# Layer 0, first phase: transposes and g's matmuls on two PSUM banks in turn instead of one

## The chip, the cores and the metric

The program runs on one core of a Trainium2 chip. The metric is the device time of one execution in microseconds (us); the profile of one execution spans 3190.1 us. The engines are named as the profile names them: PE (TensorE, with PEld for its weight loads), DVE (VectorE), ACT (ScalarE), POOL (GpSimd) and SP (SyncE, which here only issues transfers). PSUM is the memory that PE's results land in. The kernel uses eight banks of it, each a piece of 128 partitions by 512 float32 values.

## The reference

The input is 1024 images of 16 x 16 pixels with 16 channels, all in float32. Four layers follow one another, and each has the form x = x + f(groupnorm(x)), with eight groups of two channels.

```python
x = x + _L0_conv_ref(_gn(x), core0, core1, core2)   # a 4096 x 4096 matrix as a train of three cores
x = x + _L1_conv_ref(_gn(x), ...)                    # depthwise taps, dense 48 -> 128 -> 16, masks
x = x + _L2_conv_ref(_gn(x), ...)                    # 3 x 3 convolution, 16 -> 16
x = x + _L3_conv_ref(_gn(x), ...)                    # as layer 1, with other weights
```

Only layer 0 is touched by the change. Its matrix is given by three cores of ranks 1, 16, 16, 1: with `r` and `q` the inner ranks, each entry is a sum over r and q of core0[o0,i0,r] * core1[r,o1,i1,q] * core2[q,o2,i2]. The kernel forms the product of core1 and core2 once, calls it g, and then multiplies g with combinations of core0 to get the blocks of the matrix.

## The kernel before, in words

**Batches.** The 1024 images are worked in two halves of 512, n = 0 and n = 1. A tile "line" is 128 partitions (places and channels of an image) by 512 images, so it fills one bank as a matmul's result.

**Layer 0's main work.** `layer_train` computes the matrix product as a block product with seven products in place of eight (`PRODUCTS`, with sums and differences of blocks on both sides). It goes through five phases of 16 units each. A unit is one group of 128 output rows; it has some of the seven products, and each product is four matmuls of 128 x 128 by 128 x 512 that add up in one bank `po` (line 1078). Phase 0 has only two products for each unit, since only the half n = 0 is loaded and normalized when it begins; phase 1 has the five others, and the remaining phases have seven. Each product is cut in two steps, `go(0)` and `go(2)`, so phase 0 has 16 x 2 x 2 = 64 steps. Around its matmuls a step also calls work on the next units:

- `build(u + 1)` in the first step of unit u: eight matmuls from `gq` (a piece of g, from DRAM) and `R` (core0's combinations) into four banks `pw`, which ACT copies into the weights `w` (lines 1001 and 1006). DVE then forms a mixed block (line 1019).
- `store(u - 1)` and `gload(u + 2)`: transfers on SP's queue, the second brings a piece of g.
- `gather`: in phase 0 an ACT copy of `po` into `r` (line 1103).

**What is done beside phase 0.** The other half of the input must be turned: `turn` (line 821) makes four transposes of 128 x 128 into one bank `ptin`, ACT copies the bank to SBUF (lines 824 and 832), and POOL issues the transfer of the result to `xr` in DRAM. 18 such groups of the half n = 0 are left over at the start of phase 0, and 32 of n = 1 follow. Between them stand eight groups of `gs` (line 551): four matmuls into one bank `pg` that make a part of g, and an ACT copy (line 555). Two groups of `spread` (line 870, bank `ptmr`) bring the mean and the factor of the norm of n = 1 into place. POOL also issues the loads of the images of n = 1 into the slots that the turned pieces leave, in two lots of four transfers of 1 MB.

**Order.** [...] `run` emits the 64 steps of phase 0 and deals the work beside them between them by shares, so a group of transposes stands at a fixed place between two groups of matmuls on PE. ACT works in the same order of emission. [...]a group that writes into a bank waits until ACT's copy of what stood there before is done.

**Banks.** Until the end of layer 0 the eight banks are divided by tags: three for `po` (tag "o"), four for the builder (tag "w") and one shared bank (tag "m").

```python
stage(es, dict(gn, w=2, r=2, gq=2, R=1), dict(o=3, w=4, m=1))
```

The banks of a tag are given out in a ring: a new tile takes the one that was taken longest ago. The transposes and g's matmuls in phase 0 all take tag "m", so each group needs the bank of the group just before it. Before phase 0 begins (turning the first lines, g's first half) the same helpers use tag "w" alone. A build takes all four banks "w".

**Later.** Phases 1 to 4 follow, with the preparation of the weights of layers 1 and 3 (`nca_weights`, names `L_conv_...`) beside phase 1, and then layers 1 to 3. The change reaches none of their code.

A remark on counts: a float32 matmul of the code appears as two records in the trace, a transpose as one. A step's two matmuls are "po x4" in the trace, a build's eight are "pw x16", a group of g's four "pg x8", and a group of transposes "ptin x4".

Of the kernel before, what the change touches and what calls it, by code (L numbers as in the profile page):

```python
# [103 lines left out]
def conv_preact_kernel(ctx: ExitStack, tc: tile.TileContext, a: dict, out: bass.AP):  # L104
# [22 lines left out]
    def stage(es, sb, ps):  # L127

        for key, sizes, kw in (("sb", sb, {}), ("ps", ps, {"space": PSUM})):
            p = es.enter_context(  # L130
                tc.tile_pool(name=f"{key}{len(pool)}", bufs=1, reuse_waits="tile", **kw)
            )
            pool[key] = p, sizes
        pool[len(pool)] = None

    def work(shape, tag, name, dt=F32):
        p, sizes = pool["sb"]
        return p.tile(shape, dt, tag=tag, name=name, bufs=sizes[tag])

    def bank(shape, tag, name):  # L140
        p, sizes = pool["ps"]
        return p.tile(shape, F32, tag=tag, name=name, bufs=sizes[tag])

    def psum(shape, name):
# [342 lines left out]
    def train_setup(room):  # L487

        c1t = room[0:16, 0:4096].rearrange("p (h i w a k) -> p h i w a k", h=2, i=S, w=4, a=2)
        ra = [room[0:16, 4096 + 512 * a2 : 4608 + 512 * a2].rearrange("p (s m b f) -> p s m b f", s=2, m=2, b=2) for a2 in range(2)]  # L490
        c0 = room[0:16, 5888:6144].rearrange("p (i o) -> p i o", o=S)
        c1n = work([P, 2, NB], "t4", "core1")[:, 0].rearrange("p (t f) -> p t f", t=2)
        r = work([P, NB], "n", "cores")
        c2 = r[0:16, 0:256]
        c0n = r[:, 256:288].rearrange("p (t k) -> p t k", t=2)

        core1 = a["L0_conv_core1"].rearrange("k o i q -> o k (i q)")
        for h in range(2):
            for wv in range(4):
                for a2 in range(2):  # L500
                    A.dma_start(c1n[32 * wv + 16 * a2 : 32 * wv + 16 * a2 + 16, h], core1[8 * a2 + 4 * h + wv])
        A.dma_start(c2, a["L0_conv_core2"].rearrange("r o i k -> r (o i k)"))
        A.dma_start(
            c0n, a["L0_conv_core0"].rearrange("r o i k -> (r o i) k").rearrange("(t p) k -> p t k", p=P)
        )

        def cores():
            for h in range(2):
                for i2 in range(0, S, 4):
                    pt = bank([16, 4, P], "w", "pc1")  # L510
                    for j in range(4):
                        T.transpose(pt[:, j], c1n[:, h, 16 * (i2 + j) : 16 * (i2 + j) + 16], ident)
                    A.copy(c1t[:, h, i2 : i2 + 4].rearrange("p i w a k -> p i (w a k)"), pt)
            pt = bank([16, 2, P], "w", "pc0")
            for t in range(2):
                T.transpose(pt[:, t], c0n[:, t], ident)
            for t in range(2):
                A.copy(
                    c0[:, :, 8 * t : 8 * t + 8].rearrange("p i o -> p o i"),
                    pt[:, t].rearrange("p (o i) -> p o i", i=S),  # L520
                )

        def sums():
            c = c0.rearrange("p (b s t) o -> p s b (t o)", b=2, s=2)
            for a2 in range(2):
                G.memset(ra[a2], 0.0)
                G.tensor_copy(ra[a2][:, :, a2], c)
                G.dma_start(c_dram[a2], ra[a2].rearrange("p s m b f -> p (s m b f)"))

            st0["R"] = work([P, 2, 256], "R", "R")  # L530
            for g in range(4):
                G.dma_start(
                    st0["R"][32 * g : 32 * g + 32].rearrange("p s f -> p (s f)"),
                    c_dram.rearrange("a k f -> (a k) f"),
                )

        def gs(h, ih, o, ni, tag):


            if (h, ih, o) not in st0:  # L540
                if ih:
                    g = work([P, 2, NB], "t4", "g")
                else:
                    if o == 0:
                        st0["gw"] = work([P, 28, P], "w", "g")
                    g = st0["gw"][:, 8 * o : 8 * o + 8]
                st0[h, ih, o] = [g.rearrange("p m f -> p (m f)").rearrange("p (o f) -> p o f", o=8), 0]
            g, i2 = st0[h, ih, o]
            pg = bank([P, ni, 8, S], tag, "pg")
            for j in range(ni):  # L550
                T.matmul(
                    pg[:, j], c1t[:, h, 8 * ih + i2 + j].rearrange("p w a k -> p (w a k)"),
                    c2[:, P * o : P * o + P], start=True, stop=True,
                )
            A.copy(
                g[:, :, 16 * i2 : 16 * (i2 + ni)].rearrange("p o (j i) -> p j o i", j=ni), pg
            )
            st0[h, ih, o][1] += ni
            if i2 + ni == 8:
                nc.sync.dma_start(  # L560
                    g_dram[ih, 2 * h : 2 * h + 2, :, :, 8 * o : 8 * o + 8].rearrange(
                        "w v k o f -> (w v k) o f"
                    ),
                    g,
                )

        def all_gs(ih, tag):
            return [
                (1, lambda h=h, o=o: gs(h, ih, o, 4, tag)) for h in range(2) for o in range(2) for _ in range(2)
            ]  # L570

        return [cores, sums] + all_gs(0, "w"), all_gs(1, "m")

# [308 lines left out]
    def normed(p, n, src=None):  # L884

        X, E = part_tile(p)

        def op(b, t, k):
            x = X[:, b, t : t + 2, n]
            y = x if k or src is None else X[:, b, t : t + 2, src]  # L890
            m = mr[:, k, n].unsqueeze(1).broadcast_to([P, 2, NB])
            V.tensor_tensor(x, y, m, ALU.mult if k else ALU.subtract)  # L892

        return [(1.2, lambda b=b, t=t, k=k: op(b, t, k)) for b in range(2) for t in (0, 2) for k in range(2)]
# [34 lines left out]
    def part_steps(p):  # L929
        steps = load_part(p) + [10] + normed(p, 0) + normed(p, 1)  # L930
        return steps + combined(p, True) + combined(p, False)
# [528 lines left out]
    def steps_of(*more):  # L1460
        return (lambda: None), [x for m in more for x in m]

    def now(steps):
        for step in steps:
            step = step[1] if isinstance(step, tuple) else step
            if callable(step):
                step()
# [8 lines left out]
    with ExitStack() as es:  # L1476
        stage(es, dict(gn, w=2, r=2, gq=2, R=1), dict(o=3, w=4, m=1))
        setup, later = train_setup(XN[0].rearrange("p n b -> p (n b)")[:, 8192:14336])
        tag = ["w"]
        loads, stat, lines, tail = input_steps(0, tag, 0, nc.sync)  # L1480
        now(loads)

        A.activation(work([P, NB], "n", "warm")[:, 0:1], ident[:, 0:1], AF.Sqrt)
        now(setup[:1])
        now(stat[0] + stat[1])
        now(setup[1:])
        now(lines[0][:4] + lines[1][:4] + tail[:3] + lines[0][4:10] + tail[3:])
        start, phases = layer_train()
        start()
        now(normed(0, 0, 1) + combined(0, True))  # L1490
        tag[0] = "m"
        late = lines[0][10:] + lines[1][4:]
        loads, stat, lines, tail = input_steps(1, tag, 2, G)
        woven_in = [x for j in range(2) for i in range(4) for x in stat[j][i : i + 1] + lines[j][4 * i : 4 * i + 4]]
        run(
            steps_of(phases[0]), 130, (),
            (late[:6] + loads[0:4] + late[6:] + loads[4:] + later + woven_in + tail + normed(0, 1) + combined(0, False), 0.0, 1.0),
        )
        run(
            steps_of(phases[1]), 350, (),  # L1500
            (beside(make1, make3), 0.0, 0.74), (part_steps(1), 0.75, 0.98),
        )
        for i in (2, 3):
            run(
                steps_of(phases[i]), 415, (), (part_steps(i), 0.05, 0.9),
                ([lambda: conv.update(s=conv_weights()), 60, lambda: conv["s"]()] if i == 2 else [0.0], 0.0, 0.5),
            )
        nst, N = parts_cw(X0, True)
        for q in range(4):
            bg = alone(N, q - 1) if q else [0.0]  # L1510
            if q == 3:
                bg = bg + rstd(nst, slice(0, 96)) + [3] + scaled(N, range(3))
            run(
                steps_of(phases[4][56 * q : 56 * q + 56]), 104, [put(L1)] if q == 3 else (),
                (bg, 0.08, 0.95),
            )
# [66 lines left out]
```

## Time and profile before

| | |
|---|---|
| time, median of 3 runs | 3199.57 us (3197.21 to 3203.37) |
| span of the profiled execution | 3190.1 us |
| PE busy | 3058.5 us (96%) |
| DVE busy | 1785.6 us (56%) |
| ACT busy | 1018.3 us (32%) |
| POOL busy | 670.6 us (21%) |
| mean granted clock of PE | 0.98 of full |
| first matmul `po` of phase 0 | starts at 46.67 us |
| last transpose `ptin` | starts at 200.8 us |
| first transposes for phase 1's norm, `ptmr` of n = 1 | 210.32 us |

PE is the engine to watch: a microsecond in which it stands idle counts, as long as nothing else would have stopped it later. PEclk in the profile is the clock that the chip granted to PE. "Idle before" in a view is the time in which an engine stood still ahead of an instruction, with the instruction on another engine that ended the wait.

### The profile page before, as it was taken

What the parts mean: (1) busy time and instruction counts of PE and PEld (TensorE: products, weight loads), DVE (VectorE), ACT (ScalarE), POOL (GpSimd) and SP (SyncE); (2) the same over time, 40 slices, a digit from 0 to 9 for tenths busy, and PEclk for the clock granted to TensorE, in tenths of its full rate; (3) what the DMA queues carried; (4) which work ended last, traced back from release to release, by engine and by line L of the source; (5) the groups of instructions that cost most, each with busy time, mean ns of one, the idle gap of its engine ahead of it and who ended that gap; (6) DMA issues with size and microseconds to landing.
All of it is one profiled execution on the core that took longest, in us unless ns stands there. A gap on an engine that the chain in (4) does not pass through costs nothing.

```text
span 3190.1 us, 37179 instructions
## 1 busy us (share of the span) xinstructions
PE 3058.5 (96%) x13874; PEld 1260.3 (40%) x13874; DVE 1785.6 (56%) x2378; ACT 1018.3 (32%) x1690; POOL 670.6 (21%) x706
## 2 busy tenths in 40 slices
PE   7899899999999999999999999999979899999996
PEld 5444333444444444444444433333323233333332
DVE  5255345755554555544556678558757647754222
ACT  4331221100001000000111166666624356655553
POOL 1116532200000000000000034435432124432221
PEclk8999999999999999999999999999989999999998
DMA  7535545443333433322222254454476765433445
GB/s 283 201 142 97 121 101 160 133 144 104 104 109 132 146 116 104 104 98 96 90 95 90 76 168 133 129 167 154 139 192 110 185 139 173 136 92 115 128 137 186
DMA packets 243299, 424.77 MB, mean 133 GB/s; under 512 B 37844, under 2 KB 91952, under 8 KB 239408
## 3 DMA queue, kind: packets, MB, share of 16 engines
q1 hardware_dynamic: 217824, 368.63, 35.5%
q0 software_dynamic: 24480, 53.48, 8.3%
q8 instruction: 110, 1.80, 0.2%
q14 instruction: 69, 0.57, 0.1%
q10 hardware_dynamic: 816, 0.30, 0.0%
HBM read 238.78 MB, written 165.60 MB: 127 GB/s over the span
## 4 chain that ended last, share of the span: by engine, by line
issue 46%; PE 31%; POOL 8%; DMA 4%; DVE 2%; SPq 1%; ACT 1%; POOLq 0%; DVEq 0%; ACTq 0%
PE ph L1410 11%; PE po L1078 10%; PE po L1263 4%; POOL res L1313 4%; POOL u L1312 4%; PE po L1160 2%; DMA xn<-xf 1%; PE L_conv_pe L382 1%; SPq L941 1%; DVE xn L621 1%; DMA hx<-xn 1%; PE pw L1001 1%; PE ptout L948 1%; DVE sq L592 1%; POOL L_conv_wy L394 0%
## 5 line engine op out<-in xcount | busy, mean ns | idle before, releaser
L1078 PE MATMUL po<-xn,w 128*128 128x512 f32 x3584 | 1584.3, 598 | 4.6 <-DVE xn L892 4.6
L1078 PEld LDWEIGHTS po<-xn,w 128*128 128x128 f32 x3584 | 669.9, 190 | 852.6 <-issue 833.7
L1413 ACT ACTIVATE hid<-ph,pack 128x512 f32<-128x512 f32 x1024 | 653.9, 686 | 429.2 <-PE ph L1410 308.4
L1114 DVE TENSOR_TENSOR r<-r,po 128x512 f32<-128x512 f32 x576 | 377.8, 683 | 499.0 <-PE po L1078 476.3
L1312 POOL TENSOR_TENSOR u<-u,mask 128x512 f32<-128x512 f32 x128 | 202.5, 1582 | 1858.9 <-DMA nx<-xn 1241.7
L1410 PE MATMUL ph<-xn,wq 32*128 32x512 f32 x3664 | 573.1, 613 | 1.5 <-DMA wq<-L_conv_wy 1.5
L1006 ACT COPY w<-pw 128x512 f32<-128x512 f32 (+1 forms) x320 | 150.6, 558 | 1194.0 <-issue 970.4
L1410 PEld LDWEIGHTS ph<-xn,wq 32*128 32x128 f32 x3664 | 228.6, 184 | 263.3 <-issue 231.4
L1410 PE MATMUL ph<-xn,pack 32*128 32x512 f32 x1288 | 302.2, 631 | 4.5 <-ACT hid L1413 3.2
L1263 PE MATMUL po<-hid,pack 128*32 128x512 f32 x2048 | 283.0, 609 | 1.2 <-DVE u L1275 0.9
L1019 DVE TENSOR_TENSOR w<-w 128x512 f32<-128x512 f32 x320 | 211.2, 684 | 115.2 <-ACT w L1006 114.7
L621 DVE TENSOR_TENSOR xn<-xn,m 128x1024 f32<-128x1024 f32 x160 | 225.9, 1461 | 47.1 <-ACT m L636 47.1
L1313 POOL TENSOR_TENSOR res<-res,u 128x512 f32<-128x512 f32 x128 | 215.2, 1681 | 17.0 <-PE po L1263 2.7
L1275 DVE SCALAR_TENSOR_TENSOR u<-po,pack,xn 128x512 f32<-128x512 f32 x128 | 95.9, 749 | 157.6 <-PE po L1263 150.9
L1160 PE MATMUL po<-xn,convw 128*128 128x512 f32 x368 | 168.5, 609 | 0.0
L1410 PEld LDWEIGHTS ph<-xn,pack 32*128 32x128 f32 x1288 | 114.5, 187 | 100.7 <-issue 61.7
L1114 DVE TENSOR_TENSOR xn<-xn,po 128x512 f32<-128x512 f32 x96 | 64.3, 684 | 125.9 <-PE po L1078 125.8
L592 DVE TENSOR_TENSOR sq<-sq 128x1024 f32<-128x1024 f32 x78 | 110.6, 1418 | 15.2 <-ACT sq L606 12.0
L1263 PEld LDWEIGHTS po<-hid,pack 128*32 128x32 f32 x2048 | 42.9, 108 | 189.7 <-issue 137.4
L394 POOL DMA_DIRECT2D L_conv_wy<-xn x160 | 89.0, 563 | 99.0 <-ACT xn L152 90.7
L1160 PEld LDWEIGHTS po<-xn,convw 128*128 128x128 f32 x368 | 69.3, 193 | 99.3 <-issue 96.7
L592 DVE TENSOR_TENSOR s<-s,xn 128x1024 f32<-128x1024 f32 x60 | 86.4, 1441 | 29.1 <-DMA xn<-xf 27.9
(163 smaller groups left out, 1776.9 us busy)
## 6 DMA issues: line engine op xcount, KB each, us to landing
xf<-r SPq DMA_DIRECT2D x112, 512.0 KB, 3.8
xn<-xf SPq DMA_DIRECT2D x96, 512.0 KB, 5.1
r<-xf SPq DMA_DIRECT2D x80, 512.0 KB, 4.5
wq<-L_conv_wy SPq DMA_DIRECT2D x192, 192.0 KB, 2.8
res<-xf SPq DMA_DIRECT2D x128, 256.0 KB, 3.0
xf<-res SPq DMA_DIRECT2D x96, 256.0 KB, 2.0
res<-xr SPq DMA_DIRECT2D x256, 64.0 KB, 2.8
xf<-conv POOLq DMA_DIRECT2D x64, 256.0 KB, 6.1
```

The lines of the kernel that those rows point to most:

```text
L592: return lambda: V.tensor_tensor(st["t"], st["t"], p(), ALU.add)
L621: V.tensor_tensor(part, part, m().unsqueeze(1).broadcast_to([P, 2, NB]), op)
L1006: A.copy(w[:, k0:4, :, 32 * r : 32 * r + 32].rearrange("p k t (v o) -> p v (k t) o", v=2), pw[r],)
L1019: V.tensor_tensor(w[:, k], w[:, x], w[:, y], ALU.add if sign > 0 else ALU.subtract)
L1078: T.matmul(po, st["w", u][:, matrix, t], x, start=t == 0, stop=t == 3)
L1114: V.tensor_tensor(r[at], r[at], po, ALU.add if sign > 0 else ALU.subtract)
L1160: T.matmul(st["po", h][wh], conv["fw"][:, y], X[:, 16 * wh + h + y - 1], start=y == max(0, 1 - h), stop=y == min(2, S - h),)
L1263: T.matmul(po[32 * j : 32 * j + 32], nca["w1"][:, v], hid[j], start=v == 0, stop=v == 1)
L1312: G.tensor_tensor(u, u, st["m"][:, w2], ALU.mult)
L1313: G.tensor_tensor(r, r, u, ALU.add)
L1410: T.matmul(ph, w, x, start=k == 0, stop=k == len(tiles) - 1)
L1413: A.activation(h, ph, AF.Relu, bias=nca["bt"][:, r : r + 1])
```

## The change

The helper `bank` gets a new tag "mw". A request for it flips a counter and takes, in turn, one of the builder's four banks (tag "w") and the shared bank (tag "m"); the first request gets "w". The groups of `turn`, `spread` and `gs` that run beside phase 0 ask for "mw" instead of "m". So two groups in a row no longer need the same bank, and the second can be written while ACT copies the first. No bank, instruction or transfer is added or taken away, and the order on each engine stays.

```diff
+    either = [0]
+
     def bank(shape, tag, name):
         p, sizes = pool["ps"]
+        if tag == "mw":
+            either[0] ^= 1
+            tag = "mw"[either[0]]
         return p.tile(shape, F32, tag=tag, name=name, bufs=sizes[tag])
@@
-        return [cores, sums] + all_gs(0, "w"), all_gs(1, "m")
+        return [cores, sums] + all_gs(0, "w"), all_gs(1, "mw")
@@
         now(normed(0, 0, 1) + combined(0, True))
-        tag[0] = "m"
+        tag[0] = "mw"
         late = lines[0][10:] + lines[1][4:]
```

The builder's groups still ask for "w", and the preparation of the later layers' weights (`psum`) still for "m".

## The prediction

> **What bounds the kernel now.** I read the page first, then PE's waits in the stretch of phase 0, then PE's and ACT's timelines side by side, and last the transfers and the chain of waits behind the stretch.
>
> ```profile
> PE 3058.5 (96%) x13874; PEld 1260.3 (40%) x13874; DVE 1785.6 (56%) x2378; ACT 1018.3 (32%) x1690; POOL 670.6 (21%) x706
> ```
>
> PE stands idle for only 131.6 us of 3190.1. What phase 0 has of that (46 to 225 us) the waits of PE name:
>
> ```profile
> PE ptin L821 <- ACT lines L832: 13.5, 17, 1.2
> PE po L1078 <- DVE xn L892: 4.6, 1, 4.6
> PE pg L551 <- ACT g L555: 2.9, 4, 0.7
> PE ptin L821 <- ACT xn L824: 2.6, 3, 1.2
> PE pw L1001 <- DMA gq<-g_dram: 0.9, 1, 0.9
> ```
>
> Columns: total us, times, longest. Three rows are waits for the copy out of the shared bank: 13.5 + 2.9 + 2.6 = 19.0 us in 24 waits, 0.6% of the time. PE's timeline shows the two kinds:
>
> ```profile
> 125.33 0.73 PE L1001 MATMUL pw<-R,gq 32*128 32x128 f32 x16
> 125.99 0.66 PE L821 MATMUL ptin<-ident,xn 128*128 128x128 f32 x4
> 127.82 0.66 PE L821 MATMUL ptin<-ident,xn 128*128 128x128 f32 x4 [1.18 <-ACT xn L824]
> 128.31 1.88 PE L1078 MATMUL po<-xn,w 128*128 128x512 f32 x4
> 130.03 0.60 PE L821 MATMUL ptin<-ident,xn 128*128 128x128 f32 x4
> 130.47 3.60 PE L1078 MATMUL po<-xn,w 128*128 128x512 f32 x8
> 133.90 0.60 PE L821 MATMUL ptin<-ident,xn 128*128 128x128 f32 x4
> 135.23 0.66 PE L821 MATMUL ptin<-ident,xn 128*128 128x128 f32 x4 [0.73 <-ACT lines L832]
> ```
>
> And ACT's in the same place:
>
> ```profile
> 126.07 1.20 ACT L1006 COPY w<-pw 128x256 f32<-128x256 f32 x4 [1.72 <-PE pw L1001]
> 127.13 0.63 ACT L824 COPY xn<-ptin 128x512 f32<-128x512 f32 x1
> 128.51 0.59 ACT L824 COPY xn<-ptin 128x512 f32<-128x512 f32 x1 [0.75 <-PE ptin L821]
> ```
>
> The reader is to see that the group at 127.82 starts 0.06 us after the copy of the bank's former content ends (127.13 + 0.63 = 127.76), that ACT was late there because the builder's four copies stood before it, and that ACT is idle most of the time. A group that stands alone between `po` matmuls (130.03) waits for nothing.
>
> [...] 0.7 us gaps at every second group that follows another, none elsewhere. [...] from 102 to 122 us the granted clock by stretches of 4 us is 0.78, 0.80, 0.63, 0.50, 0.59, and a `po` x4 there takes 2.85 us instead of 1.88. That is where `pg` groups stand close together.
>
> **The change, part by part.**
>
> *Removed: the waits.* The idle time understates a wait, since the next group also loses its overlap with the one before. I count start to start. Unhindered, a group takes 0.44 us to the next start (130.03 to 130.47).
> - Second group of a pair, nothing before it: 14 times, steps of 1.27 to 1.37 us (133.90 to 135.23), minus 0.44: 0.83 to 0.93 each, 12.3 us in all.
> - Second group right behind a build: steps of 1.88, 1.83, 1.83, 1.83 and 1.64 (125.99 to 127.82), minus 0.44: 6.8 us.
> - g's pairs: 1.87 (95.42 to 97.29) against 1.08 unhindered (97.29 to 98.37): 0.8 each, four times, 3.2 us.
> - One group at 81.85, whose predecessor's copy waited for a transfer: 0.5 us.
>
> Sum 22.8 us; and after a blocked group the next `po` starts 0.05 us later (0.49 against 0.44), some 20 times, 1 us more: 23.8 us.
>
> *Added: waits on the builder's bank.* Requests alternate and the first gets "w", so I number the 58 groups through the timeline: odd ones get "w". The ring of "w" gives a group right behind a build the bank `pw` just written first. That bank is free at 126.07 + 0.39 (one of the four copies, median 386 ns) + 0.05, so 1.2 us after the build's start, where the group could start at 0.66: 0.53 us of wait. It hits the groups that now start at 50.68, 107.04, 138.19, 149.01 and 194.69: 5 x 0.53 = 2.7 us. Where the pair's second group gets "w" (79.11, 127.82) it could start 0.66 + 0.44 = 1.10 us behind the build: 0.1 us each. Behind the waiting group on PE only the next group and `po` are queued, and those are counted.
>
> *Moved to the builder.* A build takes all four "w" banks. The youngest was written by a group with at least one `po` x4 (1.72 us) in between; its copy ends about 0.7 + 0.6 us after the group. I cost this at nothing, hidden by `po`.
>
> *ACT.* A unit's copies are 1.2 (weights) + 2 x 0.58 (`r`) + at most six of 0.59, under 6 us in a unit that takes about 10: not a bound. `po` has three banks, so a late `r` copy stops nobody.
>
> *What transfers take back.* From 66 to 82 us the transfer engines' share is 1.0 and about 400 GB/s: POOL has issued four 1 MB loads at 61.92, behind PE's groups. The pieces `gq` of the build at 75.45, issued at 63.16, take up to 12.3 us and hold PE by 0.88. Loads and `gq` are issued behind PE's progress, and before them only 1.44 + 0.88 + 0.88 - 0.53 = 2.7 us are won; the landing moves forward by that, PE would by 2.7 + 1.8. The difference, 1.8 us, is lost. The turned lines' store issued at 69.02 lands after 12.1 us and holds ACT's copy at 81.21, but the second bank lets PE go on past it: the next "w" is free, and the next "m" is copied within 0.2 us. In the later stretches `gq` takes 2 to 4 us and is issued more than 8 us ahead, except at 118.98 (4.1 us ahead, with 2.9 at most), so I take 0.2 us there.
>
> *Sum.* 23.8 - 2.7 - 0.2 - 1.8 - 0.4 = 18.7 us at the end of phase 0.
>
> *Does it reach the end?* From 205 to 320 us PE has no wait. Then comes one of about 10 us; the chain leads there from PE:
>
> ```profile
> 317.97 1.01 PE L_conv_pe L382 x4
> 318.98 0.02 issue
> 319.00 0.02 ACTq L152
> 319.02 0.32 issue
> 319.34 0.59 ACT xn L152
> ...
> 353.62 1.93 PE L_conv_pe L382 x4
> ```
>
> In between POOL and its transfers work, but they were started by PE's matmul at 317.97, and POOL's earlier work at 281.35 by a DVE step that PE paces. So the whole chain comes earlier by the same amount. DVE's norm of n = 1 starts behind `ptmr` (PE, 210.32), and its last combination is ready at 236.0 where phase 1's third product needs it at about 239: both hang on PE's order and shift alike. Later stages are bound by PE or started by it. I take the full 18.7 us off 3199.6: 3181 us.
>
> **The rivals.**
> 1. *The gain as summed:* 3181 us. For it: all 24 waits are seen at their instruction. Against it: the count of residuals leans on a numbering by hand.
> 2. *The clock comes back too.* 20 us at a mean clock of 0.66 lose 20 x 0.34 = 6.8 us. Without the gaps, `po` has 1.72 of 3.9 us in g's pairs instead of 1.72 of 4.7[...]. Against it: a build and a pair of g make 2.9 us with few rows at work in one piece. If all of it goes: 3174 us.
> 3. *It is absorbed.* Transfers hold back everything between 61 and 82 us (5.3 us instead of 1.8), half-clock windows fall worse[...], and the chain through POOL at 320 to 353 doesn't shift. For it: POOL and the transfer queues are dense there. 12 us left without the last, near 0 with it: 3188 to 3200, with 3195 its middle.
> 4. *Slower.* If the ring made every build wait for the last groups' copies (16 x 0.7 = 11 us) and every "w" group for the builder's (29 x 0.53 = 15 us), 26 us would stand against 23.8: with the transfers' 1.8, 3204 us. Against it: only five groups stand right behind a build with "w".
>
> **How the numbers follow.** Chances: first 0.64, second 0.14, third 0.14, fourth 0.08. Faster by over 0.2% means below 3193.2: the first two and a third of the third, 0.82; within 0.2% 0.10; slower 0.08. The range goes from 3170 (second rival, with 3 us as the spread of the time of before) to 3193.
>
> **What would show it.** In the profile after: waits of `ptin` and `pg` for their own copies gone from PE; five of about 0.5 us on `w<-pw` copies in their place; the wait for `gq` at about 72 us grown to 2.5; the last `ptin` near 182 us and `ptmr` near 192 instead of 210.32; from there PE's records as before, shifted by 18 to 19 us, the POOL chain too. If `ptmr` comes early and the end doesn't, the third rival holds; if `pw` waits for `lines` copies at each build, the fourth; if `po` x4 at about 95 to 110 us takes 1.88 throughout, the second.

## The result and the profile after

| | before | after |
|---|---|---|
| time, median | 3198.39 us (3197.07 to 3203.37, 4 runs) | 3175.27 us (3171.91 to 3180.46, 4 runs) |
| ratio, with its 95% interval | | 0.9926 [0.9908, 0.9945] |
| span of the profiled execution | 3190.1 us | 3175.4 us |

The change takes 23 us off. The two profiled executions differ by only 14.7: the one of the kernel before is among its faster ones (3191.8 us as a run), and the two lost unlike amounts to a lower clock, as shown below. In the changed kernel the lines of code behind line 140 have moved by five (821 is 826, 1001 is 1006, 1006 is 1011, 1078 is 1083).

PE's busy time on the page is the same to 0.7 us, and so is the number of its instructions. So it isn't work that went, but waiting:

```profile
PE 3057.8 (96%) x13874; PEld 1262.0 (40%) x13874; DVE 1784.3 (56%) x2378; ACT 1016.6 (32%) x1690; POOL 669.9 (21%) x706
```

PE's waits between 46 and 225 us, columns as before (total, times, longest):

```profile
PE po L1083 <- DVE xn L897: 4.6, 1, 4.6
PE pw L1006 <- DMA gq<-g_dram: 2.4, 2, 1.4
PE ptin L826 <- ACT w L1011: 1.8, 4, 0.5
PE pg L556 <- ACT w L1011: 0.4, 1, 0.4
```

The 24 waits for a copy of `ptin` or `pg`, 19.0 us, are all gone. Five short ones for the builder's copies have come in their place, and the wait for the transfer of `gq` has grown from 0.9 to 2.4. PE's timeline shows what became of the place that the prediction looked at:

```profile
119.34 0.73 PE L1006 MATMUL pw<-R,gq 32*128 32x128 f32 x16
120.00 1.17 PE L826 MATMUL ptin<-ident,xn 128*128 128x128 f32 x8
121.01 1.88 PE L1083 MATMUL po<-xn,w 128*128 128x512 f32 x4
122.72 0.60 PE L826 MATMUL ptin<-ident,xn 128*128 128x128 f32 x4
123.16 3.60 PE L1083 MATMUL po<-xn,w 128*128 128x512 f32 x8
126.60 1.04 PE L826 MATMUL ptin<-ident,xn 128*128 128x128 f32 x8
127.47 1.88 PE L1083 MATMUL po<-xn,w 128*128 128x512 f32 x4
129.28 0.73 PE L1006 MATMUL pw<-R,gq 32*128 32x128 f32 x16
130.45 1.09 PE L826 MATMUL ptin<-ident,xn 128*128 128x128 f32 x8 [0.44 <-ACT w L1011]
```

The pair behind a build (120.00) is now one piece of eight transposes, 1.0 us from its start to the next `po` instead of 2.3. The pair at 126.60 takes 0.9 instead of 1.8. At 130.45 a pair whose first group has the builder's bank waits for the first `pw` copy.

**Two clocks.** The trace also records the time in which PE had half its clock (0.50 granted). A `po` x4 that lies in it takes 3.50 us instead of 1.88 (at 78.75 us in the change). To compare like with like I take the stretch from the first `po` of phase 0 to the second group of `ptmr` of n = 1, and subtract half of the half-clock time in it ("at full speed"); the rest is from there to the end, treated alike. This is an estimate: it takes PE as working all through the half-clock time. Both kernels were profiled three times:

| profile | stretch | half clock in it | at full speed | rest at full speed |
|---|---|---|---|---|
| before | 166.6 | 16.6 | 158.3 | 2929.0 |
| before, second | 169.2 | 22.9 | 157.8 | 2929.2 |
| before, third | 169.5 | 23.1 | 157.9 | 2927.0 |
| change | 151.8 | 26.4 | 138.6 | 2930.0 |
| change, second | 151.8 | 26.4 | 138.6 | 2929.5 |
| change, third | 151.8 | 26.3 | 138.6 | 2929.7 |

At full speed the stretch is 19.4 us shorter (158.0 - 138.6), the same in every pairing to 0.5 us, and the rest is what it was. The time lost to half clock comes on top. For the two profiled executions as a whole, half-clock time is 129.9 us before and 137.5 after: at full speed they are 18.5 us apart, and 3.8 us of that went to half clock, which leaves the 14.7.

### The profile page after: what moved, and what is told of

The parts are those of the page before. It is cut to its first block, busy times and chain, and to the rows that moved or that the text cites. A ratio compares the mean times of both kernels' runs of the same rounds, so it can differ in the third digit from the quotient of the medians.

```text
span 3175.4 us, 37193 instructions
## 1 busy us (share of the span) xinstructions
PE 3057.8 (96%) x13874; PEld 1262.0 (40%) x13874; DVE 1784.3 (56%) x2378; ACT 1016.6 (32%) x1690; POOL 669.9 (21%) x706
## 4 chain that ended last, share of the span: by engine, by line
issue 46%; PE 37%; POOL 7%; DMA 4%; DVE 2%; SPq 2%; ACT 1%; POOLq 0%; DVEq 0%; ACTq 0%
PE ph L1415 12%; PE po L1083 11%; PE po L1268 4%; POOL u L1317 3%; POOL res L1318 3%; PE po L1165 3%; DMA xn<-xf 1%; PE L_conv_pe L387 1%; SPq L946 1%; PE pw L1006 1%; PE ptin L826 1%; PE po L1174 1%; PE ptout L953 1%; DVE sq L597 1%; DVE xn L626 1%
```

## The experiments

Ratios are to the kernel before, measured beside each. Only the edits against the changed kernel are shown; e7 and e10 start from the kernel before.

**e1: the change again.** No edit.

> The changed kernel once more. If the gain is the removed waits alone (18.7 us as summed), the ratio to before is about 0.994. If half-clock windows of PE come back as a rule, it stays at 0.992 to 0.993 and its profile shows fewer half-clock windows in phase 0 than the kernel before (16.6 us of them between the first po and the second ptmr of n = 1); if they only fall by chance, their number in phase 0 differs from the first profile of the change (26.6 us). From the first po to the second ptmr group of n = 1: 166.6 us in the kernel before, 151.8 in the first profile of the change; after taking off half of the half-clock time, both theories want 138 to 139.

3173.95 us, 0.9932 [0.9917, 0.9947]. The stretch at full speed is 138.6 us as expected, with 26.4 us of half clock at the same places. So the half-clock times in phase 0 belong to this kernel and aren't chance, but they are more than before, not fewer: the gain isn't made by them.

**b1, b2, a1: both kernels again.** No edit.

> The kernel before, profiled again. PE's waits between the first po and the last ptmr are the same to 0.2 us (13.5, 2.9, 2.6 and 0.9 us); half-clock time there is 13.7 us or more at g's pairs (95 to 122 us) if g's pairs with gaps are its cause, and near 0 there if it falls by chance.

> As b1: a third profile of the kernel before, for how often half-clock windows stand at g's pairs with their gaps, and at 76 us behind the wait of 0.9 us for gq (none in the first).

> A third profile of the change. If the wait of 2.4 us for gq causes it, a half-clock window of 3.4 to 6.8 us stands behind that wait again, and one of up to 10.2 us at g's third pair, behind the wait of 0.44 us for the builder's copies.

One run each: 3187.12 and 3196.65 us for the kernel before, 3177.36 for the change. The waits repeat to 0.2 us but for the main `ptin` row, which is 12.7 and 12.8 instead of 13.5. At g's pairs (92 to 122 us) the mean clock is 0.77, 0.80 and 0.80 in the kernel before and 0.83 in all three profiles of the change. Behind the wait for `gq` (70 to 86 us) it is 1.00, 0.89 and 0.89 before, and 0.79 in all three of the change. Around the first build of phase 0 half clock lasts 6.8 us in the three profiles of before (42.78 to 49.61 us in the first of them), and 10.2 in the three of the change (44.45 to 54.69 in the first), where a wait of 0.49 us for the builder's copies stands right behind that build. The change thus loses less clock at g's pairs and more at the two other places.

**e4 and e5: each part alone.**

e4 leaves g's matmuls on the shared bank:

```diff
-        return [cores, sums] + all_gs(0, "w"), all_gs(1, "mw")
+        return [cores, sums] + all_gs(0, "w"), all_gs(1, "m")
```

e5 leaves the transposes there:

```diff
-        tag[0] = "mw"
+        tag[0] = "m"
```

> Only the transposes take two banks in turn; g's matmuls stay on the shared bank. Sum of the waits: 22.8 - 3.2 = 19.6 us of start-to-start time removed, so the time is about 3 us above the change and 15.5 us below before (ratio 0.995). In the profile four waits of pg for ACT's copy of about 0.7 us are back. If the clock windows around g's pairs hang on those gaps, it is up to 5 us above the change.

> Only g's matmuls take two banks in turn; the transposes stay on the shared bank. 3.2 us of waits removed, less one wait of 0.5 us behind a build: ratio 0.999. The transposes' waits stay at 13.5 + 2.6 us as before. If the clock comes back when g's pairs close up, half-clock time at 95 to 120 us falls below 13.7 us and up to 6 us more is gained (ratio 0.997).

e4: 3181.10 us, 0.9949 [0.9931, 0.9966]; at full speed 141.1 us, 2.5 more than the change. e5: 3188.09 us, 0.9969 [0.9956, 0.9981]; at full speed 154.6, 3.4 less than before. The parts (16.9 and 3.4) add up to 20.3 against 19.4 for both together. e4 shows its four `pg` waits of 2.9 us as expected, e5 its transposes' waits. e5 gains more than its waits: its interval lies below the 0.999 that those alone would make. Its clock at 92 to 122 us is 1.00, where the three profiles of before and e4 have 0.77 to 0.80. The stretches there:

```profile
70.00:86.00 16.00, 12.36 (x63) 6.54 (x61) 0.69 (x1) 6.18 (x13) 2.19 (x3) 1.00 0.91 356
92.00:122.00 30.00, 27.12 (x106) 15.94 (x106) 6.63 (x18) 8.69 (x19) 1.34 (x3) 0.77 0.67 253
```

(before), and of e5:

```profile
70.00:86.00 16.00, 13.03 (x58) 7.43 (x59) 0.69 (x1) 5.41 (x13) 2.20 (x3) 0.89 1.00 398
92.00:122.00 30.00, 28.82 (x163) 16.80 (x161) 6.70 (x19) 12.30 (x28) 2.90 (x5) 1.00 0.83 310
```

After the stretch and its length come the busy times of PE, PEld, DVE, ACT and POOL; the last three numbers are PE's clock, the transfers' share and GB/s. In the second row of each, PE's clock goes from 0.77 to 1.00 when g's pairs close up. This is one profile of e5; in the change the pairs close up too, and the clock is 0.83 there.

**e6: the builder's ring alone.**

```diff
-        tag[0] = "mw"
+        tag[0] = "w"
...
-        return [cores, sums] + all_gs(0, "w"), all_gs(1, "mw")
+        return [cores, sums] + all_gs(0, "w"), all_gs(1, "w")
```

> All groups of phase 0 beside the product take the builder's ring of four, the shared bank isn't used there. The fourth rival's cost by itself: every group right behind a build waits for the first pw copy, nine of them 0.53 us, a pair's second group there another 0.3 for the next copy, while groups with no build before them never wait. By the sum about 2.5 us slower than the change, 16 us faster than before (ratio 0.995). If builds had to wait for the groups' copies (0.7 us, up to 16 times), it is 10 us slower than the change, and pw shows waits for lines copies.

3180.13 us, 0.9949 [0.9928, 0.9971]; at full speed 140.7 us, 2.1 more than the change (2.5 expected). Its waits on the builder's copies:

```profile
PE ptin L826 <- ACT w L1011: 2.7, 6, 0.5
PE ptmr L875 <- ACT w L1011: 0.4, 1, 0.4
PE pg L556 <- ACT w L1011: 0.4, 1, 0.4
```

Eight waits instead of five (nine were expected, and at a pair's second group further ones of 0.3 us, which don't appear), and no row in which `pw` waits for a copy of `lines`: no build is held by the groups. The fourth rival's mechanism isn't there, even without the shared bank.

**e3: the shared bank behind a build.**

```diff
             k0 = 2 if m1 == 2 else 0
+            either[0] = 1
```

> The group right behind a build always takes the shared bank. If the five waits of 0.44 us for the builder's copies cost what they show, they vanish from PE's waits and the time falls by 2 to 3 us against the change (ratio to before lower by under 0.001: visible in the profile, hardly in the times). If a pair's second group then waits instead, waits of about 0.1 us on the same copies take their place. If some other wait takes over, the time is that of the change.

3170.13 us, 0.9918 [0.9904, 0.9932]; the times don't tell it from the change, as expected, the profile does. The five waits are gone; one of 0.5 us for a DVE step appears early in phase 0. At full speed 137.1 us, 1.5 less than the change (2 to 3 were expected; the new wait takes 0.5 of it). The half-clock time in the stretch falls from 26.4 to 9.8: g's pairs run at 1.00.

**e8: the loads dealt out.**

```diff
-            (late[:6] + loads[0:4] + late[6:] + loads[4:] + later + ...
+            (late[:6] + loads[0:1] + late[6:9] + loads[1:2] + late[9:12] + loads[2:3] + late[12:15] + loads[3:4] + late[15:] + loads[4:] + later + ...
```

> The change, with the first four 1 MB loads of n = 1 dealt out over the transposes of the other half of the images, instead of being issued together. If the loads hold back the pieces gq, the wait of pw for gq (2.4 us) falls to under 0.5 us, and with it PE's idle time there; the store of the turned lines issued at about 67 us lands within 6 us instead of 12. Gain against the change 2 to 3 us, and up to 3.4 us more if the half-clock window that follows the wait goes too. If the queue of SP and not the loads sets the landing of gq, the wait stays at 2.4 us and the time is that of the change.

3172.44 us, 0.9917 [0.9903, 0.993]. In the change PE was held in the middle of a build:

```profile
72.24 0.82 PE L1006 MATMUL pw<-R,gq 32*128 32x128 f32 x4
74.47 0.45 PE L1006 MATMUL pw<-R,gq 32*128 32x128 f32 x2 [1.42 <-DMA gq<-g_dram]
75.87 1.19 PE L1006 MATMUL pw<-R,gq 32*128 32x128 f32 x10 [0.94 <-DMA gq<-g_dram]
76.99 1.97 PE L826 MATMUL ptin<-ident,xn 128*128 128x128 f32 x8
78.75 3.50 PE L1083 MATMUL po<-xn,w 128*128 128x512 f32 x4
```

The `po` at 78.75 takes 3.50 us where 1.88 is usual: PE has half its clock from 75.17 to 82.00 us, so from the second of the two waits on. In e8 the same build comes without a wait, and the `po` behind it at full clock:

```profile
76.02 0.73 PE L1006 MATMUL pw<-R,gq 32*128 32x128 f32 x16
77.19 1.09 PE L826 MATMUL ptin<-ident,xn 128*128 128x128 f32 x8 [0.44 <-ACT w L1011]
78.12 1.88 PE L1083 MATMUL po<-xn,w 128*128 128x512 f32 x4
```

At full speed 136.2 us, 2.4 less than the change, about the wait for `gq`; against it stands one more wait of 0.44 us for the builder's copies, six in all. The pieces `gq` land after 6.7 to 7.4 us instead of 9.3 to 12.5, and the turned lines' store (issued at 68.80) after 5.2 instead of 12.9. The loads were the cause. The time moves less than this, and by itself isn't told from the change.

**e9: e3 and e8 together.** The two edits above.

> Both of these edits. If they are independent, PE has no wait of over 0.2 us between the first po and the last ptmr, and the time is 4 to 8 us below the change: ratio to before about 0.990 to 0.992. If the transfers only move the wait, it is that of the change.

3164.66 us, 0.9899 [0.9885, 0.9912]; at full speed 134.5 us, 4.1 less than the change, and 1.5 + 2.4 = 3.9 from the two: they are independent. But for the first `po` only the DVE wait of 0.5 us is left, where none of over 0.2 was expected, and the half clock in the stretch is 2.9 us. The median lies 9.3 us below that of the change in e1, more than the 4 to 8 expected.

**e7: a second shared bank, taken from `po`.**

```diff
-        stage(es, dict(gn, w=2, r=2, gq=2, R=1), dict(o=3, w=4, m=1))
+        stage(es, dict(gn, w=2, r=2, gq=2, R=1), dict(o=2, w=4, m=2))
```

> The kernel before, with the shared tag given a second bank that is taken from po (three to two). The groups no longer wait, nor for the builder: the same waits removed without the five of 0.53 us. If two banks for po are enough (an r copy or a DVE addition ends well before the next product but one), it is 2 us faster than the change. If not, po waits for DVE's or ACT's readers in all five phases of layer 0, over 400 products: at 0.1 us each 40 us slower than the change.

3165.83 us, 0.9898 [0.9881, 0.9915]. Two banks are enough for `po`: between 190 and 1300 us it waits for DVE twice, 1.5 us in all. At full speed the stretch is 137.5 us, 1.1 less than the change (2 were expected), with 6.0 us of half clock. One wait stands there that the change doesn't have:

```profile
77.81 0.60 PE L821 MATMUL ptin<-ident,xn 128*128 128x128 f32 x4
79.59 0.66 PE L821 MATMUL ptin<-ident,xn 128*128 128x128 f32 x4 [1.18 <-ACT lines L832]
```

ACT's copy there waits for the store of earlier lines to land, and two banks are one too few to go past it. In the change ACT is held at the same place by 1.14 us, and PE isn't: its next group on the builder's ring has a bank that is free.

**e10: e7 with the loads of e8 dealt out.** The edits of e7 and e8, on the kernel before.

> Both banks for the shared tag (po with two), and the first four loads of n = 1 dealt out. If the loads cause the wait for gq, it is gone, and with it what was left of e7's waits: 2 to 5 us below e7, ratio to before 0.988 to 0.990. If po's two banks begin to bind once PE is faster, po waits for ACT's r copies in phase 0, and the time is that of e7.

3159.08 us (3156.45 to 3159.86), 0.9878 [0.9861, 0.9894], the fastest of all. Between 44 and 182 us PE has one wait left:

```profile
PE po L1078 <- DVE xn L892: 4.5, 1, 4.5
```

At full speed the stretch is 133.3 us, 24.7 less than before and 4.2 less than in e7.

## Why the prediction was right

**The waits.** The sum was 18.7 us by the end of phase 0; at full speed it is 19.4. Its terms, one by one: the waits removed were all 24 that were counted. The five on the builder's bank came at the five groups that the numbering gave, with 0.44 to 0.49 us of idle for the 0.53 foreseen. The wait for `gq` grew to 2.4 us (2.5 foreseen), and e8 shows that the loads cause it, as argued. The store that holds ACT at 79.86 doesn't hold PE. The waits of 0.1 us at a pair's second group don't appear. By their idle time the waits that came in cost 2.2 + 1.5 = 3.7 us, where the sum took off 5.1; with the 19.4 this makes some 23 us removed (an estimate), against 23.8. So each part of the sum is right to about 1.4 us, and only errors of this size cancel in the total.

Not all of its working holds. Of the last 0.4 us in the sum the text names only 0.2 (at 118.98), and a wait of 0.9 us that loses 1.8 more would be 2.7, not 2.5. The "0.7 us gaps" are 1.0 to 1.2 where the group stands behind a build, and the wait "of about 10 us" behind 320 us is three waits, 8.5 us together, the longest 5.9. None of this changes the argument. One sign in the profile was missed: `ptmr` of n = 1 was to start near 192, 18 to 19 us earlier, and starts at 194.26, 16.1 earlier. The sum leaves the clock as it was, and between these two profiles the half clock in the stretch rose by 9.8 us.

**It reaches the end.** The rest at full speed lies between 2927 and 2930 us in all fourteen profiles, whether the stretch before takes 158 us or 133. The chain through POOL came forward as a whole; in the chain of waits of the change:

```profile
304.79 0.59 POOL L_conv_pk L322
...
337.58 1.93 PE L_conv_pe L387 x4
```

Before, the matmuls stood at 353.62, so they are 16.0 us earlier, as the second group of `ptmr` is (197.17 against 213.23). Ahead of 304.79 the chain of the changed kernel goes back through POOL and its transfers to a `po` of PE that ends at 262.22, where that of the kernel before left PE at 318.98. Both starts lie on PE, so both came forward. The third rival's absorption isn't there; of its parts only the half clock is real: in the profile of the change 6.8 us of it lie behind the wait for `gq`, and 10.2 us around the first build of phase 0.

**What was off.** The time lies 5.7 us below the 3181 forecast, near the second rival's number, but not for its reason. Some 3 us of it lie in the starting point: the forecast counted from 3199.6 us, the median of three runs, and over 28 later executions the kernel before takes 3196.5. That rival wanted the half clock at g's pairs to go; there it only fell from 13.7 us to 10.2, and behind the grown wait for `gq` it rose from 0 or 3.4 us to 6.8, and around the first build from 6.8 to 10.2. The likely reading is another. Each run lists its mean clock, so its span at full speed can be estimated as span times clock: over 28 executions of the kernel before it is 3124.7 us on average, over nine of the change 3105.8. Three and two are left out, whose product stands 8 to 13 us above the average of the others; in one of them, the profile of e1, the clock record is seen to lack its first stretch. That is 18.9 us, the sum as forecast (with all of them 17.7, and 18.8 between the medians). The other 3.2 us between the mean times of the 28 and the nine (3196.5 and 3174.5, 22.0 apart) are lost to half clock in the kernel before and not in the change: 70.2 against 67.0 us. The profiles don't show where, since between those of one kernel this loss differs by up to 11.6 us (59.8 to 71.4 before). Whether it belongs to the change stays open.

## What to carry to other kernels

Where one engine bounds the kernel and each of its short groups waits for the copy of the group before, count the waits from start to start, and give the groups a second bank: it may be borrowed from a ring that is used rarely, if its user comes with enough work in between. Here another lender was better: with the third bank of `po` (e7) the ratio is 0.9898 [0.9881, 0.9915], with the builder's ring (e1) 0.9932 [0.9917, 0.9947]. Look at which instruction the ring then puts ahead of a group; a group right behind the ring's own user gets the bank just written. And see what a faster engine runs into next: here a burst of loads, which dealt out gave two more microseconds, and a wait of 0.44 us in a row of matmuls of 16 and 32 rows, behind which PE ran at half clock for 10.2 us.

## What the runs showed of the hardware

In the change a wait of 0.44 us was followed by a loss of some 5 us in clock. A build, this wait and g's third pair make 3.1 us with no matmul of 128 rows:

```profile
101.59 0.73 PE L1006 MATMUL pw<-R,gq 32*128 32x128 f32 x16
102.75 2.05 PE L556 MATMUL pg<-cores,xn 16*128 16x128 f32 x16 [0.44 <-ACT w L1011]
104.73 2.67 PE L1083 MATMUL po<-xn,w 128*128 128x512 f32 x4
107.34 3.78 PE L556 MATMUL pg<-cores,xn 16*128 16x128 f32 x16
111.05 6.21 PE L1083 MATMUL po<-xn,w 128*128 128x512 f32 x8
```

10.2 us of half clock follow (from 105.9), some 5 us lost, in all three profiles and in e6. In e3, e9, e7 and e10, which lack that wait there and take 2.4 us for the same work, no half clock follows; e3:

```profile
101.53 0.73 PE L1007 MATMUL pw<-R,gq 32*128 32x128 f32 x16
102.08 1.95 PE L556 MATMUL pg<-cores,xn 16*128 16x128 f32 x16
103.96 1.99 PE L1084 MATMUL po<-xn,w 128*128 128x512 f32 x4
105.87 2.05 PE L556 MATMUL pg<-cores,xn 16*128 16x128 f32 x16
107.85 3.70 PE L1084 MATMUL po<-xn,w 128*128 128x512 f32 x8
```

In e5 and e8, which have it, 0 and 3.4 us followed, so it isn't certain. No run varied this wait alone, and none shows what lowers the clock; why e8 lost less, and e5 nothing, stays open. In the profiles of the kernel before and of the change the half-clock times last 3.41, 6.83, 10.24, 13.65 or, once, 17.07 us, but for the last one of each, which reaches the end of the record.

At the first build of phase 0, which begins while a half-clock time is under way, the wait of 0.49 us behind it goes with 10.2 us of half clock (the change three times, e4 and e8), and without it the time is 6.8 (b1, b2, e5 and e7). Behind the wait for `gq` of 2.0 to 2.4 us half clock follows for 6.8 us in six of seven profiles, and for 3.4 us or not at all behind one of 0.9. Behind this wait and at g's pairs the clock fell where PE was busy most of the time (in the change 13.65 of the 16 us from 70 to 86 us, and 29.56 of the 30 from 92 to 122), but with matmuls of 16 or 32 rows and gaps of 0.4 to 1.4 us between them.
